# Layer-1 weight sums on GpSimd: positions 13 to 17 of a turn left out

## The chip, the core and the metric

One core of a Trainium2 chip runs the program. TensorE (PE in the profile, its weight loads PEld) does the products, VectorE (DVE), ScalarE (ACT) and GpSimd (POOL) do elementwise work, SyncE (SP) issues every transfer of the kernel. Each engine works through its own instructions in order. The metric is device time in microseconds (us), the median of several runs.

## The reference

Two layers on 8192 tokens of 768 features, 64 tokens to a graph.

```
# layer 0, 12 heads of 64
h    = x @ W                              # per head
attn = leaky(tanh(h)@w_src + (tanh(h)@w_dst)^T), masked by adj, softmax
fo   = elu(attn @ h + b)
gate = sigmoid(x @ H_w.T + H_b)
x    = layernorm(x + gate*fo + (1-gate)*x)
# layer 1, 6 heads of 128
q, k, v = x@Wq+bq, x@Wk+bk, x@Wv+bv
x = layernorm(x + softmax(masked q k^T / sqrt(128)) v @ Wf + bf)
```

## The kernel before, in words

The tokens are cut in 32 pairs of 128-token tiles. Layer 0 takes one pair in each *turn* p = 0 to 31. Its three large products of a pair, h, gate and v (v belongs to layer 1, but is made here), are each seven block products in the place of eight; the operands are sums of quarter blocks of x or of the weights. Layer 1 then takes the pairs two by two and makes q, k and the output product with 15 block products ("wide") in the place of 18; their weight operands are sums of 2 x 256-row blocks of Wq, Wk and Wf.

Those weight sums are made ahead, in layer 0, by `sum_weights` (L341). It is a generator: it loads a block to `wacc` (L354), loads another to `wadd` (L357), adds it on GpSimd (L361; L367 where a block is only negated), goes on so for each further block, and stores `wacc` to DRAM (L370), from where layer 1 loads it. There are 72 such chains (12 of the 15 sums, two halves, three matrices) with 132 additions or negations of 128x256 elements. `wacc` and `wadd` have one buffer each, so a load waits on SyncE for the addition before it, or for the landing of the store before it.

A turn has 21 *positions*, numbered from 0. Position n issues one block product to TensorE (`step`) and then what is planned at that position for the other engines; `was` plans for the older pair, `at` for the newer one. The items are h1 h2 u4 u3 h6 g1 h5 h7 g2 g6 h4 h3 g5 g7 v1 v2 g4 v6 g3 v5 v7 (u is the rest of the v product of the turn before). What other engines are given, as far as the prediction speaks of it; t1 and t0 are the two tiles:

- position 0, 3: transposes of the probabilities (L955); 1, 3: `residual` on GpSimd (L1006), which waits for ScalarE's gate
- 2, 5: attention products; 3, 6: their division on VectorE (L992, L993)
- 4, 7: gating on VectorE (L1011, L1016, L1018); 5, 8: statistics, with one small GpSimd power each (L322); 6, 9: the normalisation, and the store of x1 (L1027); 8: loads of x
- 11, 12: `products`: tanh, VectorE's product (L878), GpSimd's product (L879), for t1 and then t0
- 13, 14: `terms`: VectorE's reduction (L886) and three small transfers (L888, L891), and `with_bias`: GpSimd's addition (L902) and two transfers (L907, L908)
- 15, 16, 19: VectorE's sums of x1 (`value_sums`, L240 to L243, tile `sv_v`), the second of which (L241) is the operand of the product v6 at position 17
- 16, 18: logits on VectorE (L915), 18 and 20: masking and maximum (L931, L937, L938)
- 17: GpSimd's sums of the next pair's x (`x_sums`, the same lines L240 to L243, tile `sx_x`)

The additions of `sum_weights` are put among this in turns 2 to 30: after the acts of a position the generator is advanced once at even and twice at odd positions (L1188 to L1190). An addition comes three steps after its load. In this way they fall on all positions, and the work is done in turn 24.

In the trace a turn is told by its first product with the name `x_h` (h2, position 1). "Time 35.2 of a turn" is us after that.

Of the kernel before, what the change touches and what calls it, by code (L numbers as in the profile page):

```python
# [9 lines left out]
F32 = mybir.dt.float32  # L10
# [3 lines left out]
ALU = mybir.AluOpType  # L14
AX = mybir.AxisListType

P = 128
# [117 lines left out]
def kernel(  # L135
# [21 lines left out]
    nc = tc.nc  # L157
    NP = x.shape[0]
    NG = NP // 2
    SCALE = 1.0 / math.sqrt(E1)  # L160
    W2 = PAIR * P
# [8 lines left out]
    V, S, G, T = nc.vector, nc.scalar, nc.gpsimd, nc.tensor  # L170
# [134 lines left out]
    def step(job, i):  # L305
        job.product(i)
        flush()
        behind.append((job, i))
# [32 lines left out]
    def sum_weights(pool):  # L341

        for key, src in (("q", wq), ("k", wk), ("f", wf)):
            for n, (_, blocks, *_) in enumerate(WIDE):
                if blocks[0][2] > 0 and len(blocks) == 1:
                    continue
                for kc in range(2):

                    def block(k, f):
                        r0 = (2 * k + kc) * P  # L350
                        return src[r0 : r0 + P, f * W2 : (f + 1) * W2]

                    acc = pool.tile([P, W2], F32, tag="wacc", name=f"wacc_{key}{n}_{kc}", bufs=1)
                    nc.sync.dma_start(out=acc, in_=block(*blocks[0][:2]))  # L354
                    for k, f, sign in blocks[1:]:
                        t = pool.tile([P, W2], F32, tag="wadd", name=f"wadd_{key}{n}_{kc}_{k}{f}", bufs=1)
                        nc.sync.dma_start(out=t, in_=block(k, f))  # L357
                        yield
                        yield
                        yield  # L360
                        G.tensor_tensor(acc, acc, t, ALU.add if sign > 0 else ALU.subtract)  # L361
                    if blocks[0][2] < 0:
                        assert len(blocks) == 1
                        yield
                        yield
                        yield
                        G.tensor_scalar(acc, acc, -1.0, None, ALU.mult)  # L367
                    yield
                    yield
                    nc.sync.dma_start(out=wide_d[key][n][:, kc, :], in_=acc)  # L370
                    yield
                    yield

    def wide_place(key, n):
# [362 lines left out]
    def drain(*sides):  # L737
        for s in sides:
            for _ in s:
                pass  # L740
# [4 lines left out]
    with ExitStack() as ph, ExitStack() as ph_r:  # L745
        sb = ph.enter_context(tc.tile_pool(name="sb0", bufs=2))
# [346 lines left out]
            jobs["rows"] = rows  # L1093

        v_sums, carried = {}, {}
        summing = sum_weights(sb)
        for p in range(NP + 1):
            q = p - 1
            new, old = p < NP, 0 <= q < NP
# [84 lines left out]
            for pos, item in enumerate(turn):  # L1184
                step(jobs[item[0]], int(item[1:]))
                for act in plan.get(pos, ()):
                    act()
                if 2 <= p < NP - 1:  # L1188
                    for _ in range(1 + pos % 2):
                        next(summing, None)  # L1190
                if item[0] == "q":
                    jobs["rows"].ready(int(item[1:]) + 4)
            if p == NP - 2:
                drain(summing)
            if old:
                jobs["u"] = jobs["v"]
        flush()
# [3 lines left out]
    with ExitStack() as ph:  # L1201
        sb = pools["late"] = ph.enter_context(
            tc.tile_pool(name="sb1", bufs=2, reuse_waits="tile")
        )
# [42 lines left out]
        for g in range(1, NG):  # L1247
# [26 lines left out]
            p = 2 * g - 2  # L1274
# [7 lines left out]
        p = 2 * NG - 2  # L1282
# [66 lines left out]
```

## Time and profile before

| what | us |
|---|---|
| median of 4 runs (2899.89 to 2903.07) | 2901.36 |
| the profiled execution | 2899.93 |
| its span, first to last instruction | 2898.1 |
| TensorE busy (98% of the span) | 2843.1 |
| VectorE busy (67%) | 1936.2 |
| GpSimd busy (45%) | 1292.2 |
| ScalarE busy (37%) | 1060.4 |
| the 126 additions L361, by matrix q, k, f | 36.4, 36.1, 35.9 |
| TensorE waiting for L241 of VectorE, whole span | 8.6 in 9 waits |

Busy time is the time in which an engine ran instructions; "idle before" is the time for which it stood still, with the instruction whose end released it. The granted TensorE clock is 0.996 of full speed. Layer 0 takes about the first 1540 us, a turn some 46.

### The profile page before, as it was taken

The page shows a single profiled execution, that of the slowest core. Times are in us where ns is not written, and L with a number is a line of the kernel's source. Part 1 is how long each engine was busy: PE and PEld are TensorE (multiplying, and loading weights), DVE is VectorE, ACT ScalarE, POOL GpSimd, SP SyncE. Part 2 cuts the span into 40 slices and gives each one's busy share as a digit, 9 for nine tenths or more (in the row PEclk, how much of TensorE's full clock was granted, in tenths as well). Part 3 has the DMA queues.
Part 4 walks back from the last instruction along what each step waited for, and adds up shares of the span by engine and source line. Part 5 has one row for each costly group of instructions (what it writes and reads, how often), then busy time and mean ns, then how long its engine had stood idle before and what let it go on. Part 6 is the DMA issues. An engine that isn't in the chain of part 4 may idle for free.

```text
span 2898.1 us, 47864 instructions
## 1 busy us (share of the span) xinstructions
PE 2843.1 (98%) x18252; PEld 2074.7 (72%) x18252; DVE 1936.2 (67%) x3201; ACT 1060.4 (37%) x1896; POOL 1292.2 (45%) x1253
## 2 busy tenths in 40 slices
PE   7899999999999999999999999999999999999998
PEld 4566556666566655666668888888888888888886
DVE  6888788888878888887874545555545555554556
ACT  2344444444444444444433123333213333322332
POOL 2434454444535444333443454444545443444534
PEclk9999999999999999999999999999999999999999
DMA  5344444544444444333353434332334333233432
GB/s 175 119 156 149 149 142 144 159 146 147 143 153 147 140 148 134 120 121 104 121 201 84 124 101 110 106 92 75 87 81 111 110 101 91 72 84 95 110 88 74
DMA packets 321780, 348.73 MB, mean 120 GB/s; under 512 B 147856, under 2 KB 246672, under 8 KB 321552
## 3 DMA queue, kind: packets, MB, share of 16 engines
q1 hardware_dynamic: 321552, 345.66, 39.1%
q8 instruction: 146, 2.39, 0.4%
q14 instruction: 82, 0.67, 0.1%
HBM read 198.48 MB, written 122.29 MB: 111 GB/s over the span
## 4 chain that ended last, share of the span: by engine, by line
PE 82%; DVE 10%; DMA 3%; ACT 2%; issue 2%; POOL 1%; SPq 0%; POOLq 0%; DVEq 0%; ACTq 0%
PE z_k L442 9%; PE z_o L489 8%; PE z_q L442 8%; PE y_h L270 7%; PE y_g L270 6%; PE y_k L442 6%; PE y_v L270 6%; PE y_o L489 6%; PE y_q L442 5%; PE z_h L270 4%; PE z_v L270 3%; PE z_g L270 2%; PE x_g L270 2%; PE sp L545 2%; PE cp L629 2%
## 5 line engine op out<-in xcount | busy, mean ns | idle before, releaser
L569 ACT ACTIVATE sc<-sc 128x512 f32<-128x512 f32 x48 | 30.7, 639 | 615.2 <-DVE sc L566 615.2
L690 POOL TENSOR_TENSOR y<-y,bf_bc 128x768 f32<-128x768 f32 x64 | 114.7, 1814 | 290.1 <-DMA y<-x1d 290.1
L502 DVE TENSOR_TENSOR y<-y,z_o 128x256 f32<-128x256 f32 x320 | 127.3, 418 | 139.3 <-PE z_o L489 139.0
L489 PE MATMUL z_o<-wf,so 128*128 128x256 f32 x896 | 215.8, 383 | 1.6 <-DVE y L502 1.6
L442 PE MATMUL z_q<-xs,w_wq 128*128 128x256 f32 x896 | 213.5, 381 | 0.3 <-POOL xs L406 0.3
L406 POOL TENSOR_TENSOR so<-ctxT 128x256 f32<-128x256 f32 x224 | 159.8, 732 | 91.2 <-PE y_o L489 46.5
L442 PE MATMUL z_k<-xs,hw_wk 128*128 128x256 f32 x840 | 198.5, 379 | 0.0
L1006 POOL TENSOR_TENSOR x<-gate,x 128x768 f32<-128x768 f32 x64 | 119.6, 1869 | 162.4 <-ACT gate L1057 148.3
L442 PEld LDWEIGHTS z_q<-xs,w_wq 128*128 128x128 f32 x896 | 168.7, 190 | 24.3 <-POOL xs L406 0.7
L489 PEld LDWEIGHTS z_o<-wf,so 128*128 128x128 f32 x896 | 167.1, 190 | 26.0 <-DVE y L502 1.4
L322 POOL TENSOR_TENSOR rs_b<-ve_b,minus_half 128x1 f32<-128x1 f32 x64 | 40.4, 631 | 314.8 <-DVE ve_b L320 313.0
L879 POOL TENSOR_TENSOR th<-th,wsd 128x768 f32<-128x768 f32 x64 | 117.2, 1832 | 140.3 <-DVE th L878 140.3
L442 PEld LDWEIGHTS z_k<-xs,hw_wk 128*128 128x128 f32 x840 | 159.5, 190 | 21.7
L322 POOL TENSOR_TENSOR rs_a<-ve_a,minus_half 128x1 f32<-128x1 f32 x64 | 35.8, 560 | 305.7 <-DVE ve_a L320 305.7
L406 POOL TENSOR_TENSOR xs<-r,r 128x512 f32<-128x512 f32 x112 | 147.6, 1334 | 39.7 <-DMA r<-x1Td 22.5
L457 DVE TENSOR_TENSOR qT<-qT,z_q 128x512 f32<-128x512 f32 x96 | 66.0, 687 | 141.7 <-PE z_q L442 140.7
L270 PE MATMUL y_v<-wv,sv_v 128*128 128x384 f32 x384 | 136.3, 491 | 10.3 <-DVE sv_v L241 8.6
L270 PE MATMUL y_h<-w_wq,xT 128*128 128x384 f32 x384 | 136.5, 492 | 8.7 <-DMA w_wq<-in_w_dram 8.0
L457 DVE TENSOR_TENSOR kT<-kT,z_k 128x512 f32<-128x512 f32 x96 | 66.0, 688 | 112.5 <-PE z_k L442 110.4
L270 PE MATMUL y_h<-w_wq,sx_x 128*128 128x384 f32 x384 | 136.5, 492 | 4.2 <-ACT h L839 4.2
L270 PE MATMUL y_g<-hw_wk,sx_x 128*128 128x384 f32 x384 | 136.4, 492 | 2.5 <-DVE hw_wk L219 2.2
L270 PE MATMUL z_v<-wv,sv_v 128*128 128x384 f32 x384 | 137.5, 494 | 1.0 <-DVE v L869 1.0
(163 smaller groups left out, 6912.8 us busy)
## 6 DMA issues: line engine op xcount, KB each, us to landing
x<-in_x_dram SPq DMA_DIRECT2D x64, 384.0 KB, 3.7
dd<-dstd SPq DMA_DIRECT2D x128, 192.0 KB, 3.4
x1d<-x SPq DMA_DIRECT2D x64, 384.0 KB, 2.6
x1Td<-x1T SPq DMA_DIRECT2D x32, 768.0 KB, 4.2
vd<-v SPq DMA_DIRECT2D x64, 384.0 KB, 3.1
r<-x1Td SPq DMA_DIRECT2D x96, 256.0 KB, 3.5
v<-vd SPq DMA_DIRECT2D x384, 64.0 KB, 2.3
y<-x1d SPq DMA_DIRECT2D x64, 384.0 KB, 5.7
```

Of the source, the lines that this page charges most:

```text
L270: T.matmul(to[:, : self.n], lhsT, rhs, start=kc == 0 and not more, stop=kc == HK - 1, skip_group_check=more,)
L322: G.tensor_tensor(rstd, ve, minus_half, ALU.pow)
L406: G.tensor_tensor(t, self.of(x[0]), self.of(x[2]), x[1])
L442: T.matmul(b[:, half * W2 : (half + 1) * W2], w[:, kc, half * P : (half + 1) * P], x[:, kc, :], start=half == kc == 0 and not more, stop=k ...
L457: V.tensor_tensor(at, at, b.rearrange("p (h t) -> p h t", h=2), ALU.add if sign > 0 else ALU.subtract,)
L489: T.matmul(b[:, :W2], x[:, kc, :], w[:, kc, :], start=kc == 0 and not more, stop=kc == 1, skip_group_check=more,)
L502: V.tensor_tensor(at, at, self.banks[path][:, :W2], ALU.add if sign > 0 else ALU.subtract)
L545: T.matmul(self.sp_[gr * N : (gr + 1) * N, (i * 2 + a) * N : (i * 2 + a + 1) * N], qT[:, 2 * self.f + a, at], kT[:, 2 * self.f + a, at], s ...
L629: T.matmul(self.cp_[a][e, at], self.v_[rows, i, gr, e], self.scT_[rows, at], start=True, stop=True,)
L690: G.tensor_tensor(y, y, pools["bf"], ALU.add)
L879: G.tensor_tensor(th[:, 1, :], th[:, 1, :], wsd[:, 1, :], ALU.mult)
L1006: G.tensor_tensor(xp, st[t]["gate"], xp, ALU.mult)
```

## The change

`sum_weights` now asks before each addition whether it may: it stays in `while not (yield)` until the turn sends it true. The turn sends once at every position, and false at 13 to 17. The step after the addition issues the store, the next one the load of the following block; before, each of these came two steps later. A negation goes through the same loop. The first load is issued ahead of turn 0.

```diff
-                    for k, f, sign in blocks[1:]:
-                        t = pool.tile([P, W2], F32, tag="wadd", ...)
-                        nc.sync.dma_start(out=t, in_=block(k, f))
+                    for k, f, sign in blocks[1:] or [(None, None, -1)]:
+                        if k is not None:
+                            t = pool.tile([P, W2], F32, tag="wadd", ...)
+                            nc.sync.dma_start(out=t, in_=block(k, f))
                         yield
+                        while not (yield):
+                            pass
+                        if k is None:
+                            G.tensor_scalar(acc, acc, -1.0, None, ALU.mult)
+                        else:
+                            G.tensor_tensor(acc, acc, t, ALU.add if sign > 0 else ALU.subtract)
                         yield
-                        yield
-                        G.tensor_tensor(acc, acc, t, ALU.add if sign > 0 else ALU.subtract)
-                    if blocks[0][2] < 0:
-                        assert len(blocks) == 1
-                        yield
-                        yield
-                        yield
-                        G.tensor_scalar(acc, acc, -1.0, None, ALU.mult)
-                    yield
-                    yield
                     nc.sync.dma_start(out=wide_d[key][n][:, kc, :], in_=acc)
-                    yield
                     yield
...
-        summing = sum_weights(sb)
+        summing, summed = sum_weights(sb), False
+        next(summing)
...
-                if 2 <= p < NP - 1:
-                    for _ in range(1 + pos % 2):
-                        next(summing, None)
+                if 2 <= p < NP - 1 and not summed:
+                    try:
+                        summing.send(not 13 <= pos <= 17)
+                    except StopIteration:
+                        summed = True
...
-                drain(summing)
+                assert summed
```

Counted from the two programs, the 132 additions stand behind these positions:

| position | 0 | 1 | 2, 3 | 4 | 5, 6 | 7 | 8 | 9 | 10 | 11 | 12 | 13 to 17 | 18 | 19, 20 | last turn |
|---|---|---|---|---|---|---|---|---|---|---|---|---|---|---|---|
| before | 5 | 10 | 15 | 3 | 10 | 11 | 5 | 9 | 4 | 7 | 4 | 36 | 2 | 11 | 24 |
| after | 9 | 18 | 1 | 20 | 6 | 13 | 11 | 3 | 6 | 13 | 5 | 0 | 27 | 0 | 29 |

The numbers of additions, loads and stores are the same, and without those the order of every engine's instructions is unchanged.

More of the change, by code (lines that the diff above doesn't have):

```diff
@@ L354, in sum_weights @@
                     nc.sync.dma_start(out=acc, in_=block(*blocks[0][:2]))
-                    for k, f, sign in blocks[1:]:
-                        t = pool.tile([P, W2], F32, tag="wadd", name=f"wadd_{key}{n}_{kc}_{k}{f}", bufs=1)
-                        nc.sync.dma_start(out=t, in_=block(k, f))
+                    for k, f, sign in blocks[1:] or [(None, None, -1)]:
+                        if k is not None:
+                            t = pool.tile([P, W2], F32, tag="wadd", name=f"wadd_{key}{n}_{kc}_{k}{f}", bufs=1)
+                            nc.sync.dma_start(out=t, in_=block(k, f))
                         yield
-                        yield
-                        yield
-                        G.tensor_tensor(acc, acc, t, ALU.add if sign > 0 else ALU.subtract)
-                    if blocks[0][2] < 0:
-                        assert len(blocks) == 1
-                        yield
-                        yield
-                        yield
-                        G.tensor_scalar(acc, acc, -1.0, None, ALU.mult)
-                    yield
-                    yield
+                        while not (yield):
[4 more added lines that the diff above has]
+                            G.tensor_tensor(acc, acc, t, ALU.add if sign > 0 else ALU.subtract)
+                        yield
                     nc.sync.dma_start(out=wide_d[key][n][:, kc, :], in_=acc)
-                    yield
                     yield
```

## The prediction

> **What bounds the kernel now.** I read the shares, then TensorE's waits, then single turns. TensorE is busy for 98% of the span. Its waits between 120 and 1440 us, where the change acts:
>
> ```profile
> PE 2843.1 (98%) x18252; PEld 2074.7 (72%) x18252; DVE 1936.2 (67%) x3201; ACT 1060.4 (37%) x1896; POOL 1292.2 (45%) x1253
> ...
> PE y_v L270 <- DVE sv_v L241: 7.8, 8, 1.7
> ```
>
> So the product v6 waits for VectorE's second sum of x1 in eight turns. What the weight sums cost in all shows by the turn's length. The table by stretches has a turn without sums (number 29), and two with them (23 and 22):
>
> ```profile
> 1348.22:1393.83 45.61, 45.61 (x249) 27.68 (x247) 36.92 (x55) 20.01 (x33) 16.53 (x14) 1.00 0.34 113
> 1074.04:1119.72 45.68, 45.63 (x249) 27.72 (x247) 36.83 (x54) 20.13 (x33) 27.18 (x24) 1.00 0.46 148
> 1026.99:1074.04 47.05, 45.77 (x248) 27.68 (x247) 38.61 (x56) 20.00 (x33) 20.22 (x18) 1.00 0.47 147
> ```
>
> First the length, then PE, PEld, DVE, ACT, POOL. All turns from 25 on take 45.6 us. Turns 3 to 24 reach from 152.04 to 1165.78 us: 1013.74 - 22 x 45.60 = **10.5 us lost to the sums**. Turn 2 has one between its two L902 (0.73 us) ahead of a 1.36 us wait; I add 0.7. The sums thus cost 11.2 us, and no change of their places can bring more.
>
> Next, what makes v6 late. The timeline of turn 29, no sums (start, us, engine):
>
> ```profile
> 1376.48 1.81 POOL L879 TENSOR_TENSOR th<-th,wsd 128x768 f32<-128x768 f32 x1 [0.89 <-DVE th L878]
> ...
> 1378.25 3.34 POOL L902 TENSOR_TENSOR h<-h,b_bc 128x768 f32<-128x768 f32 x2
> ...
> 1380.70 1.31 DVE L240 TENSOR_TENSOR sv_v<-x1T 128x384 f32<-128x384 f32 x1
> ...
> 1381.53 1.33 POOL L240 TENSOR_TENSOR sx_x<-xT 128x384 f32<-128x384 f32 x1
> 1382.04 1.24 DVE L241 TENSOR_TENSOR sv_v<-sv_v,x1T 128x384 f32<-128x384 f32 x1
> ...
> 1383.42 2.17 PE L270 MATMUL y_v<-wv,sv_v 128*128 128x384 f32 x6
> ```
>
> VectorE's L240 ends 0.42 us after L902 (1381.59), its L241 0.42 after GpSimd's own L240: each finishes only when the GpSimd instruction beside it has ended. v6 starts 0.14 us after L241, at time 35.20 of the turn. So there is no slack: what delays L902 delays v6. Turn 17 has an addition at position 12, ahead of L902:
>
> ```profile
> 826.69 0.73 POOL L361 TENSOR_TENSOR wacc_f<-wacc_f,wadd_f 128x256 f32<-128x256 f32 x1
> ...
> 827.37 3.33 POOL L902 TENSOR_TENSOR h<-h,b_bc 128x768 f32<-128x768 f32 x2
> ...
> 830.65 1.32 POOL L240 TENSOR_TENSOR sx_x<-xT 128x384 f32<-128x384 f32 x1
> 831.15 1.23 DVE L241 TENSOR_TENSOR sv_v<-sv_v,x1T 128x384 f32<-128x384 f32 x1
> ```
>
> Its v6 starts at 832.53, time 36.02: 0.82 late. But turn 3, with an addition at position 11 between the two L879, is on time (187.25, time 35.21):
>
> ```profile
> 179.38 1.45 POOL L361 TENSOR_TENSOR wacc_q<-wacc_q,wadd_q 128x256 f32<-128x256 f32 x1
> 180.80 1.81 POOL L879 TENSOR_TENSOR th<-th,wsd 128x768 f32<-128x768 f32 x1
> 182.57 3.33 POOL L902 TENSOR_TENSOR h<-h,b_bc 128x768 f32<-128x768 f32 x2
> ...
> 186.35 0.56 DVE L241 TENSOR_TENSOR sv_v<-sv_v,x1T 128x384 f32<-128x384 f32 x1
> ...
> 194.69 0.73 POOL L361 TENSOR_TENSOR wacc_q<-wacc_q,wadd_q 128x256 f32<-128x256 f32 x1 [8.79 <-DMA wadd_q<-in_wq_dram]
> 195.38 1.31 POOL L240 TENSOR_TENSOR sx_x<-xT 128x384 f32<-128x384 f32 x1
> ```
>
> L902 ends 0.5 us late there too (185.90, time 33.86 against 33.37). But the addition of position 16 waits for its load 8.79 us, and **holds GpSimd's sums of x, queued behind it, away from VectorE's L241**, which takes 0.56 us in the place of 1.24. A hold of 2 us or more stands ahead of L240 in most turns with an addition at 15 or 16; the change takes it away.
>
> **The change, part by part.** Counts are those of the issue order; no instruction is added.
>
> (1) Removed: 36 additions at 13 to 17, and all old places. The 11.2 us go; each new place is priced in the turns of before that have the same one.
>
> (2) 13 additions at position 11 (7 before). L879 of t0 starts 0.47 us late (time 28.75 in turn 3, 28.28 in the row above), so do L902 and, with no hold, v6: 13 x 0.47 = **6.1 us**. Ends: 0 (turn 3) and 0.82 (turn 17). I take 0.47, since in every new turn GpSimd's L240 stands directly behind L902, as in turn 29.
>
> (3) 5 at position 12 (4 before): 0.75, between the addition's 0.73 and turn 17's 0.82: **3.8 us**. Ends 0 and 4.1.
>
> (4) Late loads. Position 11's load is issued at 9, behind the x1 store that waits for ScalarE (SyncE, time 22.6), and in seven turns behind the landing of the store of position 8 as well. Of the six additions at 11 of turns 3 to 24, two waited:
>
> ```profile
> 1056.68 0.73 POOL L361 TENSOR_TENSOR wacc_f<-wacc_f,wadd_f 128x256 f32<-128x256 f32 x1 [1.50 <-DMA wadd_f<-in_wf_dram]
> ```
>
> and 0.3 us in turn 14. Behind it are queued L879, both L902 and the x sums; VectorE's L886, SyncE's L907 and v6 wait for these. Mean (1.5 + 0.3) / 6 = 0.3; 13 x 0.3 = **3.9 us**. Ends: none late, 0; all by the mean of the two, 0.9, 11.7.
>
> (5) Pairs at positions 1 and 4: 12 turns. The first pushes L1006 of t0 onto VectorE's L1011, the second falls on L1016. In turn 8 (additions at 388.92 and 391.91) these take 1.83 and 1.37 us in the place of 1.34 and 0.96; the normalisation, and behind it on ScalarE the tanh, come later, and L878 starts at time 24.98, 0.28 later than 24.50 plus the 0.2 by which this turn was already late. Turns 14, 16 and 19 show the same 0.28, and L879 follows. 12 x 0.28 = **3.4 us**, ends 0 and 3.4. The eight additions at 4 without one at 1 fall behind L1006, as in turn 15 (0.04, nothing).
>
> (6) 9 at position 0, one round trip (2.2 us) behind the addition of 18, so some 2.1 us before the next turn's first x_h, where VectorE runs L915. It matters because L938 of t0 ends at 2.28 of the next turn, and ScalarE's exponentials and gate, VectorE's divisions and TensorE's second transposes follow without slack: turn 24, with an addition 1.67 us before its x_h, ends L938 0.45 late and is 0.47 longer. Turn 18, with one 1.96 us before, shows 0.01. I take 0.05: **0.5 us**; ends 0 and 4.1.
>
> (7) 27 at position 18, directly behind GpSimd's L243, which ends at time 40.46. The 0.73 us lie beside VectorE's L937 (40.5 to 41.5), a reduction that takes 0.95 us with or without GpSimd beside it. **0**. Without that cover it would fall on L938, by turn 24 0.45 us each: upper end 12.2.
>
> (8) The rest: positions 5 to 10 stand beside VectorE's small operations, and their successors on GpSimd (L322) come 2 us or more later; 0. SyncE's stores and loads at 12 to 14 stand between the two tiles' small transfers; turn 18 has the same two loads there, and its logits did not wait. The 17 stores at 19 and loads at 20 stand ahead of the loads of xT and adj, as in turn 8, where xT had 25 us to spare. The early first load is one 0.33 us issue: 0.
>
> The sum: 6.1 + 3.8 + 3.9 + 3.4 + 0.5 = 17.7, less 11.2: **+6.5 us**. The profiled execution would take 2899.9 + 6.5 = 2906.4 (its span 1.8 less); the median, 1.4 above it, **2907.9**.
>
> The row for the contention is L240's end 0.42 us after L902's. The Trainium skill (SBUF — State Buffer, "Who interferes with whom") says that a VectorE instruction with two SBUF inputs contends with any GpSimd instruction that reads SBUF, and that the second to issue blocks until the first has finished. That speaks against the change: emptied positions still hold L902 and the x sums, which block just as well. By that rule alone the 18 additions at 11 and 12 would each cost their whole 0.73 us, 13.1 in the place of 9.9; I keep the rows.
>
> **Rivals.** (A) Loads come in time and pairs cost nothing: 6.1 + 3.8 + 0.5 - 11.2 = -0.8, **2900.6**. For it: four of six additions at 11 did not wait. Against: four turns of four show the pair's 0.28. (B) The other side, not slower but faster: the x sums begin late without a hold. The place is GpSimd's L240, the price all of (2), (3) and (5): 3.9 + 0.5 - 11.2 = -6.8, **2894.6**. It decides from L240 at time 34.5 or later, when VectorE's L241 is through. What could do it is a late xT load, which moves behind the store of position 19; against it: in turn 8 it landed at time 8.0, 25 us early. (C) The additions of 18 start late, and fall on L938: 17.7 + 12.2 - 11.2 = +18.7, **2920**. Against: their loads are issued at 11 to 16; the margin to L938 is only 0.4 us.
>
> **How the numbers follow.** The forecast's own range is 2902 to 2914 (the late loads of (4) between 0 and 0.8 each), chance 0.58; A 0.22, B 0.08, C 0.12. A measurement of this kernel can tell about 0.2%, 5.8 us. Above 2907.2 lie 0.36 of the forecast and C: slower 0.48. Within: 0.22 of it and A: 0.44. Faster: B, 0.08. The range for 8 in 10 reaches into A and part of C: 2899 to 2918.
>
> **What would show it.** Right: in turns with an addition at 11 or 12 v6 starts 0.5 to 0.8 us after 35.2, with GpSimd's L240 directly behind L902; turns without (12, 21) take 45.6; L241 is still what TensorE waits for most. (4) is right if some L361 ahead of L879 still wait for a load, (5) if L878 slips by 0.28, (7) if L938 beside position 18 stays at 0.96. Wrong: v6 on time in those turns, or waits at the transposes in every turn.

## The result, and the profile after

The changed kernel takes **2905.3 us** (median of 33 runs, 2902.11 to 2907.9) against 2900.77 of the kernel before (53 runs beside it on the same chips): a ratio of 1.0015, 95% interval 1.001 to 1.002. It is slower by 4.5 us: the interval leaves out 1, so the loss is clear of noise, though it is below the 0.2% that the prediction took for the limit of what can be told. The forecast was 2907.9, range 2899 to 2918; of its three outcomes (slower, within 0.2%, faster) "within", held at 0.44, came true, and not "slower", held at 0.48.

The profiled execution took 2907.7 us. Its page has the same shares; VectorE's busy time is 17 us longer, TensorE's 2 us:

```profile
PE 2845.5 (98%) x18252; PEld 2074.2 (71%) x18252; DVE 1952.9 (67%) x3201; ACT 1059.7 (36%) x1896; POOL 1282.3 (44%) x1253
```

What TensorE waits for between 120 and 1440 us (total, times, longest):

```profile
PE y_v L270 <- DVE sv_v L241: 13.2, 23, 1.2
PE pTp L951 <- DVE fo L989: 0.5, 3, 0.2
```

Before, v6 waited in 8 turns, up to 1.7 us; now it waits in 23, at most 1.2. The changed file is four lines shorter up to here, so L898 is the old L902, L875 the old L879, L874 L878, L911 L915, L934 L938, L951 L955, L989 L993, and L365 is the addition. Turns 3, 18, 17, 12 and 30 by stretches (length, then PE, PEld, DVE, ACT, POOL):

```profile
150.51:196.59 46.08, 45.77 (x248) 27.70 (x247) 38.07 (x55) 20.02 (x33) 20.70 (x18) 1.00 0.44 133
566.87:612.94 46.07, 45.86 (x249) 27.61 (x247) 37.85 (x55) 20.05 (x34) 19.29 (x18) 1.00 0.49 153
798.00:844.71 46.71, 45.76 (x249) 27.70 (x247) 38.81 (x55) 19.98 (x33) 20.16 (x19) 1.00 0.45 141
844.71:890.98 46.27, 45.75 (x249) 27.70 (x247) 38.06 (x55) 20.01 (x33) 19.90 (x19) 1.00 0.43 139
1399.55:1445.16 45.61, 45.61 (x249) 27.70 (x248) 36.91 (x55) 20.01 (x33) 16.54 (x14) 1.00 0.30 97
```

Turn 30 has no sums left and takes 45.61, as before. Turn 3 has an addition at 11, turn 18 one at 12; these lose 0.47 and 0.67. Turns 17 and 12 lose by what the sum had put at nothing. Turn 18 in the timeline:

```profile
874.74 0.72 POOL L365 TENSOR_TENSOR wacc_k<-wacc_k,wadd_k 128x256 f32<-128x256 f32 x1
...
875.42 3.33 POOL L898 TENSOR_TENSOR h<-h,b_bc 128x768 f32<-128x768 f32 x2
...
878.70 1.31 POOL L240 TENSOR_TENSOR sx_x<-xT 128x384 f32<-128x384 f32 x1
879.19 1.23 DVE L241 TENSOR_TENSOR sv_v<-sv_v,x1T 128x384 f32<-128x384 f32 x1
...
880.57 1.85 PE L270 MATMUL y_v<-wv,sv_v 128*128 128x384 f32 x5 [0.52 <-DVE sv_v L241]
```

GpSimd's L240 stands directly behind L898, VectorE's L241 ends 0.42 us after it, and v6 starts at time 35.86, 0.66 late. Turn 17 shows the first thing that was missed, an addition of position 10 that waits 3.81 us for its load, with L875 queued behind it:

```profile
824.00 0.73 POOL L365 TENSOR_TENSOR wacc_k<-wacc_k,wadd_k 128x256 f32<-128x256 f32 x1 [3.81 <-DMA wadd_k<-in_wk_dram]
824.68 1.81 POOL L875 TENSOR_TENSOR th<-th,wsd 128x768 f32<-128x768 f32 x1
825.11 2.19 DVE L874 TENSOR_TENSOR th<-th,wsd 128x768 f32<-128x768 f32 x1 [0.91 <-ACT th L873]
```

Turn 12 shows the second. The addition of position 18 of turn 11 waits for its load and falls beside VectorE's L911, which takes 1.99 us (1.52 without):

```profile
563.54 0.78 POOL L365 TENSOR_TENSOR wacc_k<-wacc_k,wadd_k 128x256 f32<-128x256 f32 x1 [1.82 <-DMA wacc_k<-in_wk_dram]
563.64 1.99 DVE L911 TENSOR_TENSOR att<-dd,sd 128x768 f32<-128x768 f32 x1
```

### The profile page after: what moved, and what is told of

Its sections match the earlier page's. It is cut to its first block, busy times and chain, and to the rows that moved or that the text cites. A ratio compares the mean times of both kernels' runs of the same rounds, so it can differ in the third digit from the quotient of the medians.

```text
span 2905.9 us, 47839 instructions
## 1 busy us (share of the span) xinstructions
PE 2845.5 (98%) x18252; PEld 2074.2 (71%) x18252; DVE 1952.9 (67%) x3201; ACT 1059.7 (36%) x1896; POOL 1282.3 (44%) x1253
## 4 chain that ended last, share of the span: by engine, by line
PE 82%; DVE 11%; ACT 3%; DMA 2%; issue 1%; POOL 1%; SPq 0%; POOLq 0%; DVEq 0%; ACTq 0%
PE z_o L485 8%; PE z_k L438 8%; PE z_q L438 8%; PE y_h L270 8%; PE y_v L270 6%; PE y_k L438 6%; PE y_o L485 6%; PE y_q L438 5%; PE y_g L270 5%; PE z_h L270 4%; PE z_v L270 4%; DVE sd L882 3%; PE z_g L270 2%; PE x_g L270 2%; PE cp L625 2%; PE sp L541 2%
## 5 line engine op out<-in xcount | busy, mean ns | idle before, releaser
L322 POOL TENSOR_TENSOR rs_b<-ve_b,minus_half 128x1 f32<-128x1 f32 x64 | 40.4, 631 | 314.2 <-DVE ve_b L320 312.4
L322 POOL TENSOR_TENSOR rs_a<-ve_a,minus_half 128x1 f32<-128x1 f32 x64 | 35.9, 561 | 315.4 <-DVE ve_a L320 307.5
L875 POOL TENSOR_TENSOR th<-th,wsd 128x768 f32<-128x768 f32 x64 | 117.2, 1831 | 124.9 <-DVE th L874 124.9
L270 PE MATMUL z_h<-w_wq,sx_x 128*128 128x384 f32 x384 | 137.6, 495 | 0.6 <-DVE w_wq L216 0.6
```

The lines of the kernel that those rows point to most:

```text
L270: T.matmul(to[:, : self.n], lhsT, rhs, start=kc == 0 and not more, stop=kc == HK - 1, skip_group_check=more,)
L322: G.tensor_tensor(rstd, ve, minus_half, ALU.pow)
L875: G.tensor_tensor(th[:, 1, :], th[:, 1, :], wsd[:, 1, :], ALU.mult)
```

## The experiments

Eleven runs. Medians compare only within runs on one chip (the kernel before stands at 2900.6, 2900.7 and 2897.4 in the three sets), so the ratio is given; it is estimated from all the runs and lies up to 0.0006 off the quotient of the medians. Beside it stands, from each one's trace, by how much turns 3 to 29 exceed 27 x 45.60 us, and the length of turn 2. What lies outside these turns differs by some 3 us either way between executions. The column is one execution each: turns 3 to 24 of the kernel before, which three dose runs below contain unchanged, exceed by 10.5, 12.4, 11.9 and 10.7 us in the four traces, so a difference under 2 us in it shows nothing.

| kernel | median, us | ratio to before, 95% interval | turns 3 to 29 over 45.60 | turn 2 |
|---|---|---|---|---|
| before | 2900.77 | 1 | 10.6 | 48.3 |
| after | 2905.3 | 1.0015 (1.001 to 1.002) | 17.8 | 48.1 |
| e1_all: nothing closed | 2895.45 | 0.9986 (0.9977 to 0.9994) | 8.4 | 47.6 |
| e2_no11: 11 to 17 closed | 2900.37 | 1.0001 (0.9993 to 1.001) | 11.5 | 50.8 |
| e3_hold: after, x sums held | 2894.65 | 0.9978 (0.9969 to 0.9986) | 6.5 | 48.2 |
| e4_bhold: before, x sums held | 2898.55 | 0.9993 (0.9984 to 1.0002) | 11.3 | 48.3 |
| e7_noload: after without loads | 2903.35 | 1.0013 (1.0004 to 1.0022) | 15.4 | 48.1 |
| e8_cheap: cheap positions alone | 2895.36 | 0.9983 (0.9974 to 0.9992) | 3.1 | 49.5 |
| e10_cheap3: the same from turn 3 | 2889.2 | 0.9973 (0.9964 to 0.9982) | 2.7 | 47.6 |
| e11_cheap3_hold: and x sums held | 2882.66 | 0.9955 (0.9942 to 0.9967) | -1.8 | 47.6 |

### The closing undone, and made wider

```diff
-                        summing.send(not 13 <= pos <= 17)
+                        summing.send(True)                      # e1_all
...
-                        summing.send(not 13 <= pos <= 17)
+                        summing.send(not 11 <= pos <= 17)       # e2_no11
+                        if pos == 6:
+                            summing.send(True)
```

> The changed kernel with the turn sending true at every position, so the pace and the spacing of loads and stores stay those of the change and only the closing of positions 13 to 17 is undone. Additions per position 8 3 9 6 7 8 3 9 5 6 6 7 6 6 8 2 9 8 4 5 7, done in turn 24. Theory (the time is set by what stands ahead of or beside GpSimd's L902 and x sums, and additions at 15 and 16 that wait for their load hold the x sums off): fewer additions at 11 (7 for 13), holds are back, six turns fewer are touched; about the time of the kernel before, 2899 to 2903. Rival (the closer spacing, or one step a position, is what costs): stays at 2904 to 2907.

> The changed kernel with positions 11 to 17 closed in the place of 13 to 17, and a second step at position 6 so that the sums still end in turn 29 (14 13 0 5 17 6 16 8 4 8 13 additions at 0 to 10, 28 at 18). Theory: the 18 additions ahead of L902 are gone, which took 6.0 + 3.4 us and 0.8 for late loads in the trace; 13 in the place of 6 stand at position 10, where late loads took 0.4 us each, and 7 pairs in the place of 12 at 0.28 us: -10.2 + 2.8 - 1.4, about 2896 (2892 to 2900), faster than the kernel before. VectorE's L241 keeps GpSimd's L240 beside it (1.23 us). Rival (what counts is only that 13 to 17 are closed, or the number of turns with sums): 2903 to 2907.

Measured: 2895.45 and 2900.37. **The change has two parts of opposite sign.** Its new pace (one step a position, the store and the next load two steps earlier) with nothing closed gains 5 us; closing 13 to 17 then costs 9.9. The traces have 9.4 of this in turns 3 to 29; of the gain of the pace they show 2.2, little more than the spread between executions. Both theories had e1_all too slow. Closing 11 and 12 as well gives 4.9 back, half of what was forecast. By the traces turns 3 to 29 gain 6.3, and turn 2 loses 2.6, where an addition waits 4.57 us for its load ahead of both L875. The additions go to position 10 and before, and wait for loads there; the text had priced that at position 10 alone. In turn 6 an addition of position 7 waits 8.66 us, with GpSimd's small power L322 queued behind it:

```profile
315.91 0.73 POOL L365 TENSOR_TENSOR wacc_q<-wacc_q,wadd_q 128x256 f32<-128x256 f32 x1 [8.66 <-DMA wadd_q<-in_wq_dram]
...
316.64 0.55 POOL L322 TENSOR_TENSOR rs_a<-ve_a,minus_half 128x1 f32<-128x1 f32 x1
```

The normalisation behind L322 is late, L898 ends at 35.95 in the place of 33.37, and the turn takes 48.19.

### The loads taken away

```diff
+        acc = pool.tile([P, W2], F32, tag="wacc", name="wacc", bufs=1)
+        nc.sync.dma_start(out=acc, in_=wq[:P, :W2])
+        t = pool.tile([P, W2], F32, tag="wadd", name="wadd", bufs=1)
+        nc.sync.dma_start(out=t, in_=wq[:P, W2 : 2 * W2])
         for key, src in (("q", wq), ("k", wk), ("f", wf)):
...
-                    acc = pool.tile(...)
-                    nc.sync.dma_start(out=acc, in_=block(*blocks[0][:2]))
...
-                            t = pool.tile(...)
-                            nc.sync.dma_start(out=t, in_=block(k, f))
```

> The changed kernel without the loads of the weight sums: both buffers are loaded once ahead of the turns, and the 132 additions and 72 stores stand at their places but add the same block over and over, so layer 1 gets other weights. The theory: what goes is only the lateness of loads, about 2.4 us at position 10, 0.8 at position 11 and 0.9 at position 18 in after: 2905.3 - 4.1 = 2901.2, range 2899.5 to 2903; turns 7, 8, 16 and 17 lose 0.7 each, turns 12 and 21 go to 45.60. Rival: the lateness is covered or the place costs, and the time stays at 2904 to 2906.

Measured: 2903.35, 2 us below after, between the two expectations. The ratios, 1.0013 and 1.0015, cannot tell the two kernels apart; the traces have turns 3 to 29 shorter by 2.4. The turns say why (turns 12 and 17 here):

```profile
566.16:611.79 45.63, 45.63 (x249) 27.74 (x248) 37.40 (x55) 20.02 (x33) 19.26 (x18) 1.00 0.38 126
796.72:842.58 45.86, 45.78 (x249) 27.74 (x248) 37.97 (x55) 19.98 (x33) 20.63 (x19) 1.00 0.36 119
```

Turn 17 falls from 46.71 to 45.86, turn 12 from 46.07 to 45.63. Added up over the nine turns that become shorter, from one execution of each kernel: 1.9 us for late loads at position 10 (turns 7, 8, 16, 17), 0.9 at 11 (turns 19, 22, 23), 0.9 at 18 (turns 12, 21). But 1.3 us come back in turns 5, 11, 14, 20, 25 and 29, and some 0.5 in turns 7 and 16, which 1.9 is already less by. There the turn before has an addition at 18, and the next one is planned at position 0 of the turn itself. With its load late (2.6 us after the first behind turn 10 of after) the second lies beyond L934 of t1; without loads it follows at once and falls on it (1.25 us in the place of 0.96). **A late load costs ahead of L875 and saves behind the x sums.**

### The price of a place by itself

Into the turns 25 to 30 of the kernel before, which have no sums and take 45.60, single multiplications that wait for nothing were put (0.61 us each, where an addition of the sums takes 0.73):

```diff
+                for _ in range({25: (11,), 26: (12,), 27: (10,), 28: (1, 4), 29: (18,), 30: (5,)}.get(p, ()).count(pos)):
+                    dose = sb.tile([P, W2], F32, tag="wacc", name=f"dose_{p}_{pos}", bufs=1)
+                    G.tensor_tensor(dose, wsd[:, 1, :W2], wsd[:, 1, :W2], ALU.mult)
```

> The kernel before, with one GpSimd multiplication of 128x256 that waits for no load put into each of the turns 25 to 30, which have no weight sums and take 45.60 us each; its product is used by nothing. Turn 25 has it at position 11, 26 at 12, 27 at 10, 28 one each at 1 and 4, 29 at 18, 30 at 5. The theory (the place alone costs, as priced from the turns of after): 46.07 for turn 25, 46.31 for 26, 45.60 for 27, 45.88 for 28, 45.60 for 29 and for the turn that follows it, 45.60 for 30. The rival to the late loads of position 10: the place itself costs there, and turn 27 takes 46.0 or more without any load. Of position 18: 46.07 in the turn after 29 if the addition falls on the subtraction L938 even when it is not late.

> As the kernel before it, other places: turn 25 at position 13 (between the two bias additions L902), 26 at 14 (between the second of them and GpSimd's sums of x), 27 at 1 alone, 28 at 4 alone, 29 at 11 and 12, 30 two at 14. The theory: 46.33 for turn 25 (the whole 0.73 on the way of L902); 45.4 for 26 and 45.38 for 30, less than 45.60, since the sums of x begin 0.7 and 1.4 us later and VectorE's second sum of x1 has less or nothing beside it; 45.60 for 27 and 28; 46.8 for 29 (0.47 and 0.73). Rival: an instruction at 14 blocks VectorE's second sum as the sums of x do, and 26 takes 45.6 to 46.3; positions 1 or 4 alone cost 0.1 to 0.28.

| placed at | turn's length | cost | expected cost |
|---|---|---|---|
| 11 | 45.97 | 0.37 | 0.47 |
| 12 | 46.18 | 0.58 | 0.71 |
| 13, between the two L902 | 46.17 | 0.57 | 0.73 |
| 10 | 45.60 | 0 | 0 |
| 18 (and the next turn) | 45.61, 45.60 | 0 | 0 |
| 5; 4 alone | 45.60; 45.62 | 0 | 0 |
| 1 and 4 | 45.64 | 0.04 | 0.28 |
| 1 alone, in the turn after the one with 14 | 45.47 | not of position 1, see below | 0 |
| 14; two at 14 | 45.52; 45.53 | -0.1 | -0.2 |
| 11 and 12 | 45.58 | 0 | 1.2 |

Position 10 costs nothing by itself: its price in after is the lateness of loads. An instruction at 14, ahead of the x sums, even gains, since it holds them off VectorE's L241 (0.85 us in the place of 1.24). The gain of the next turn, with a dose at 1, is of the same source: its L938 of t0 ends at time 1.96 (the turn begins at 1257.30), before that dose has run:

```profile
1258.30 0.96 DVE L938 TENSOR_TENSOR att<-att,mx 128x768 f32<-128x768 f32 x1
```

In turn 29 of the kernel before, undisturbed, it ends at 2.28 (the turn begins at 1348.22):

```profile
1349.54 0.96 DVE L938 TENSOR_TENSOR att<-att,mx 128x768 f32<-128x768 f32 x1
```

So one at 14 gains 0.08 in its own turn and 0.13 in the next, together the 0.2 that were expected; what position 1 costs alone this run does not show. The pair at 1 and 4 comes out small, as far as the rows tell because the dose is shorter: L1011 and L1016 take 1.72 and 1.25 us beside it, 1.83 and 1.37 beside the additions of after's turn 26, which is 0.28 long.

The last row was the surprise: two instructions ahead of L902 cost nothing, where one costs 0.4 to 0.6. That turn (29) in the timeline:

```profile
1378.79 0.60 POOL L1193 TENSOR_TENSOR dose<-wsd 128x256 f32<-128x256 f32 x1
...
1379.36 3.65 POOL L902 TENSOR_TENSOR h<-h,b_bc 128x768 f32<-128x768 f32 x2
...
1380.87 0.59 DVE L240 TENSOR_TENSOR sv_v<-x1T 128x384 f32<-128x384 f32 x1
...
1381.50 1.92 DVE L241 TENSOR_TENSOR sv_v<-sv_v,x1T 128x384 f32<-128x384 f32 x1
```

VectorE's L240 is issued at 1380.87, just before the first L902 ends (some 1.68 us after 1379.36, at 1381.04), and is through 0.42 us after that end. L241 is then blocked by the second L902, not by GpSimd's L240. In an undisturbed turn L240 is issued at time 32.48, after the first L902 has ended at 31.72, so it sits out the second, and L241 sits out one more. If this is right, two at 12 must cost less than one:

> The kernel before, with GpSimd multiplications of 128x256 that wait for no load (0.61 us each, product used by nothing) in turns 25 to 30: turn 25 one at position 12, 26 two at 12, 27 three at 12, 28 two at 13, 29 two at 11, 30 one at 11 and one at 12. The theory after turn 29 of the dose run before it, where 11 and 12 together cost nothing: VectorE's two sums of x1 each end 0.42 us after the end of a GpSimd instruction, and what counts is which two ends these are. Without doses they are the ends of the second L902 and of GpSimd's L240. Where the first L902 ends after VectorE's L240 is issued (time 32.5; undisturbed it ends at 31.7), they are the ends of the first and the second L902, and nothing more of L240. So: 46.2 for one at 12, 45.4 to 45.6 for two at 12, 46.0 to 46.2 for three (the second L902 is 1.8 late, 0.5 more than a GpSimd L240), 45.4 to 45.6 for two at 13 and for 11 with 12, and 46.5 to 46.8 for two at 11, since there L879 is late, VectorE's L886 waits for it and its L240 is issued only after the first L902. Rival, each addition costs its time ahead of v6: 46.2, 46.8, 47.4, 46.8, 46.6, 46.6.

Measured in the order of that text: 46.17, 45.92, 46.60, 45.90, 46.66, 45.58. Two at 12 cost 0.32 where one costs 0.57; two at 13 cost 0.30; two at 11 cost 1.06, three at 12 cost 1.00. Against the rival, a second instruction at 12 or 13 makes the turn shorter, and two at 11 cost their full time, as the theory has it. Three sizes (two at 12, three at 12, two at 13) are 0.3 to 0.6 higher than forecast. The two doses with the gap between them take 1.31 us, where I had put 1.2, and the two L902 behind them take 3.64 in the place of 3.34: the second ends 1.6 late, 0.3 more than a GpSimd L240 lasts. Two at 12 (turn 26):

```profile
1240.31 1.31 POOL L1193 TENSOR_TENSOR dose<-wsd 128x256 f32<-128x256 f32 x2
...
1241.58 3.64 POOL L902 TENSOR_TENSOR h<-h,b_bc 128x768 f32<-128x768 f32 x2
...
1242.75 0.94 DVE L240 TENSOR_TENSOR sv_v<-x1T 128x384 f32<-128x384 f32 x1
1243.72 1.92 DVE L241 TENSOR_TENSOR sv_v<-sv_v,x1T 128x384 f32<-128x384 f32 x1
1245.19 1.31 POOL L240 TENSOR_TENSOR sx_x<-xT 128x384 f32<-128x384 f32 x1
```

L241 ends at 1245.64, 0.42 us after the second L902 (1245.22), before GpSimd's L240 has done half.

### GpSimd's sums of x held back

A GpSimd instruction of 128x1, which reads VectorE's second sum of x1, was put ahead of the x sums, so that these cannot start before L241 has ended; in after (e3_hold) and in the kernel before (e4_bhold):

```diff
         def x_sums(p):
+            if p >= 4:
+                held = small.tile([P, 1], F32, tag="rstd", name=f"held_{p}")
+                G.tensor_tensor(held, B[p - 2][6][:, 0, :1], minus_one, ALU.mult)
             operands, steps = sums_of(G, sbr, "sx", xTs[p], f"x{p}")
```

> The changed kernel with a hold made on purpose: ahead of GpSimd's sums of x, from turn 3 on, one GpSimd instruction of 128x1 that reads a column of VectorE's second sum of x1 (its result is not used). GpSimd's L240 can then not stand beside VectorE's L241. Theory: L241 takes 0.56 us in the place of 1.23, v6 starts 1.14 us after L902's end and never before 35.05, so the additions at 11 and 12 cost 0 to 0.2 in the place of 0.5 to 0.75, and every turn gains 0.15; VectorE's later chain is earlier by up to 0.3 us. About -14 - 4: 2887 (2883 to 2893). Rival (the hold does not matter; the additions cost because they delay L902, whatever follows): v6 still late by 0.5 to 0.75 in those turns, 2903 to 2908.

> The kernel before with the same hold. Theory: of its 10.5 us most stand in turns where the x sums ran directly behind L902; these go, and 0.15 in each turn: about 2890 (2886 to 2894), and the change would then bring next to nothing on top: within 3 us of e3. Rival: no gain, 2899 to 2903; or, if positions 13 to 17 cost in themselves, clearly slower than e3.

Measured: 2894.65 and 2898.55. e3_hold gains 10.7 us on after, so rival B's mechanism is real, but both stay 8 us above what was expected. e4_bhold's 2 us are not clear of noise (the interval reaches 1.0002), and its text's rival, no gain, is nearer: in its trace turns 3 to 24, where additions held the x sums in most turns already, exceed by 12.4 us, no less than without the hold. With the x sums held in both, the change is by the medians 3.9 us faster than the kernel before, not slower. e3_hold's waits of TensorE:

```profile
PE pTp L951 <- DVE fo L989: 3.5, 20, 0.2
PE y_v L270 <- DVE sv_v L241: 1.4, 2, 1.2
```

v6 hardly waits any more, and L241 takes 0.56 us. In the place of that wait 20 turns now have one of 0.17 at the next turn's transposes, the end of VectorE's chain L242, L911, L934 and the exponentials. Turn 9 of e3_hold:

```profile
459.55 0.56 DVE L241 TENSOR_TENSOR sv_v<-sv_v,x1T 128x384 f32<-128x384 f32 x1
...
460.33 1.00 POOL L240 TENSOR_TENSOR sx_x<-xT 128x384 f32<-128x384 f32 x1
460.50 1.25 DVE L242 TENSOR_TENSOR sv_v<-x1T 128x384 f32<-128x384 f32 x1
...
461.67 2.24 DVE L911 TENSOR_TENSOR att<-dd,sd 128x768 f32<-128x768 f32 x1
```

The held x sums lie on L242 (1.25 us; 0.88 in the undisturbed turn). A turn of the kernel before without sums still gains: 45.38 in turns 25 to 28 of e4_bhold.

### Cheap positions alone, and with the hold

```diff
-                if 2 <= p < NP - 1 and not summed:
+                if 3 <= p < NP - 1 and not summed:              # e10_cheap3, e11_cheap3_hold; not e8_cheap
                     try:
-                        summing.send(not 13 <= pos <= 17)
+                        summing.send(pos in (0, 1, 2, 5, 6, 7, 8, 9, 18, 19, 20))
+                        if pos in (2, 6, 19):
+                            summing.send(True)
```

e11_cheap3_hold has the edit of e3_hold too.

> The changed kernel with additions at positions 0, 1, 2, 5 to 9 and 18 to 20 alone, and a second step at 2, 6 and 19, so that the 132 additions still end in turn 29 (counted: 13 at 0, 1 at 1, 22 at 2, 20 at 5, 8 at 6, 7 at 7, 19 at 8, 2 at 9, 27 at 18, 13 at 20; no turn with a pair at 1 and 4). The theory: of the 17.8 us by which after's turns 3 to 29 exceed 45.60 only the late loads ahead of 18 and some at 0 and 8 are left, about 3: 2905.3 - 15 = 2890, range 2887 to 2895, faster than both kernels. Rival: loads come late at 8 and 9, with GpSimd's small power L322 and both L879 queued behind them as in the run with 11 to 17 closed, and the time is 2896 to 2902.

> As the run with the cheap positions alone (2895.36), but the sums begin in turn 3, not 2, and end in turn 30. The theory: turn 2 took 49.52 there, since its addition waited 5.7 us for its load ahead of both L879; without sums it takes 47 to 48.3, and one more turn at the end costs 0: 2892.5 to 2895. Rival: turn 2 is set by something else, and the time stays at 2895 to 2896.

> The same, and GpSimd's sums of x wait for VectorE's second sum of x1, as in the other run with a hold. If v6's wait alone bound the turn, each of turns 3 to 30 would go from 45.6 to 45.38: 2894 - 6 = 2888. The theory after the two runs with a hold, that VectorE's chain from its sums of x1 to L938 and the next turn's transposes has no slack either: the held sums of x and the additions of 18 behind them fall on L242, L915 and L938, TensorE waits 0.17 at the transposes in most turns, and the time is 2892 to 2896, no better than without the hold.

Measured: 2895.36, 2889.2 and 2882.66 (the last of 5 runs, the others of 11). The turns 3 to 29 of e8_cheap cost 3.1 us in all, as forecast; its median is 0.4 above the range, and turn 2 is 1.4 longer than in after (49.5 against 48.1); starting in turn 3 takes that away (47.6). The chip of the last two has the kernel before 3.3 lower, so e10_cheap3's 2889.2 answers to some 2892.5 beside the expectation, and e11_cheap3_hold's 2882.66 to some 2886.

e11_cheap3_hold went against the theory that I had formed from e3_hold and with the other reading in that text (2888), and is the **fastest of all: 14.8 us below the kernel before**. Its waits, and its turn 12:

```profile
PE y_v L270 <- DVE sv_v L241: 1.3, 2, 0.7
PE pTp L951 <- DVE fo L989: 0.5, 3, 0.2
```

```profile
561.76:607.15 45.39, 45.39 (x249) 27.80 (x247) 37.13 (x55) 20.02 (x33) 20.23 (x18) 1.00 0.40 129
```

Most turns take 45.38 with an addition at 18 in them. So VectorE's chain to the transposes does have slack when the x sums are held, just little. In e3_hold the second L898 ends between times 33.5 and 34.7, mostly after 34.0, and the transposes wait in 20 turns and more; in e11_cheap3_hold it ends between 33.2 and 33.7 in all turns but one, and they wait in six, 0.05 to 0.18. As these two runs have it, the late L898, and not the held sums by themselves, used the slack up. That is a reading of two traces, not tested by a run of its own, and it is not all: in e11_cheap3_hold turn 4 waits 0.17 behind an L898 that ended at 33.46, and turn 10 does not behind one at 33.71.

## Why the prediction was right

The sum was +6.5 us; 4.5 were measured by the medians, and in the traces turns 3 to 29 exceed 45.60 by 17.84 where the prediction had 17.7 for all new places. That agreement is partly luck, as the terms show, and closer than one execution can tell.

- (1) The old places' 11.2 us: 10.5 in turns 3 to 24 stand, the lowest of four executions (10.5 to 12.4). Of the 0.7 in turn 2 only 0.2 came (48.32 to 48.13), since an addition stands ahead of the L902 there again, between the two L875 (1.45 us).
- (2) Position 11: right. Turns 3 and 5 take 46.08 and 46.07, 0.47 each. (The reading "28.28" is 28.26 by the row that it points at, so 0.49 in the place of 0.47, 0.3 us in the sum.)
- (3) Position 12: 0.66 to 0.71 in turns 9, 11, 18, 20 and 27, 3.4 in all against 3.8.
- (4) Late loads at position 11 is **the term that failed**: 3.9 forecast, 0.7 measured in after's trace (0.9 by e7_noload). The mean of two waits in six turns of before was carried to 13 turns without asking which of them would delay L879. Six of the 13 additions waited, and the three that waited 0.4 to 0.7 us cost nothing. Turns 3 and 5 show why, the first with no wait, the second with one:

```profile
177.54 1.17 DVE L874 TENSOR_TENSOR th<-th,wsd 128x768 f32<-128x768 f32 x1 [1.08 <-ACT th L873]
...
177.85 1.44 POOL L365 TENSOR_TENSOR wacc_q<-wacc_q,wadd_q 128x256 f32<-128x256 f32 x1
...
269.98 1.16 DVE L874 TENSOR_TENSOR th<-th,wsd 128x768 f32<-128x768 f32 x1 [1.08 <-ACT th L873]
...
270.74 0.98 POOL L365 TENSOR_TENSOR wacc_q<-wacc_q,wadd_q 128x256 f32<-128x256 f32 x1 [0.42 <-DMA wadd_q<-in_wq_dram]
```

  Both additions end 0.58 us after VectorE's L874 does. An addition on time takes 1.44 us there, not 0.73, and the wait only shortens that. In turns 19, 22 and 23 it starts at L874's end or later, takes 0.72 to 0.73, and ends 0.3, 0.2 and 0.1 later than an addition on time would.
- (5) Pairs: right, 0.28 (turn 26: 45.88).
- (6) Position 0: 0.1 to 0.4 in four turns of nine, 0.9 in all against 0.5. The addition came 2.3 to 3.8 us behind that of 18, not 2.2; where it started 1.4 to 1.8 us ahead of the next turn's x_h it could fall on VectorE's L243 (0.80 us at the end of turn 28, 0.54 free) and delay L934.
- (7) Position 18: 25 of 27 cost nothing, beside the reduction, as forecast. Two came 1.5 and 1.8 us late (turns 20 and 11), fell on L911 and cost the next turn 0.47 each; nearly rival C's mechanism, in 2 turns and not 27. So turns 12 and 21, named as a sign with 45.6, took 46.07.
- (8) "Positions 5 to 10 ... 0" **failed for position 10**: the place is free (the dose), the loads are not. All six additions there waited, 1.65 to 3.85 us, and four turns lost 2.4 by it (0.7 in turn 7, 0.45 in 8 and 16, 0.8 in 17). It is not the x1 store of (4): the load is issued ahead of that store, directly behind the two loads of x, as in turn 17 (which begins at 798.00):

```profile
816.07 2.02 SPq L759 DMA_DIRECT2D x<-in_x_dram  x2
818.18 0.38 SPq L358 DMA_DIRECT2D wadd_k<-in_wk_dram  x1
821.52 0.33 SPq L1023 DMA_DIRECT2D x1d<-x  x1
```

  In the six turns it landed 0.3 us after the second load of x (1.2 in one), 3.5 to 5.7 us after its own issue, where the loads for position 11 took 2.1 to 4.5.

The miss of (4), 3.2 too much, and those of (6), (7) and (8), 0.4, 0.9 and 2.4 too little, nearly cancel, and so the sum held. One reading of the range does not come out: with no late loads the forecast is 2904.0, not the 2902 given as its lower end.

Of the rivals, A (loads in time, pairs free) fell on the pairs and on the loads of position 10. B (x sums late without a hold) did not happen by itself, but the hold showed its mechanism: with it after is faster than before.

The reason given for the loss stands: closing 13 to 17 (9.9 us between e1_all and after) moves additions from places that hold the x sums to places that delay L902 with the x sums directly behind. That turns 25 to 29 have sums too is not the cause: e8_cheap's sums end in turn 29 as well, and its turns 3 to 29 lose 3.1. The Trainium skill (SBUF — State Buffer, "Summary: rules for kernel authors") says that of a VectorE instruction with two inputs in SBUF, the on-chip memory, and a GpSimd one that reads SBUF the second to issue blocks until the first has finished. The dose runs agree: L240 and L241 each end 0.42 us after the end of a GpSimd instruction. But the estimate by that rule alone, each addition at 11 and 12 at its whole 0.73, is too high: they cost 0.47 and 0.69, and a dose at 11 with one at 12 nothing.

Left open: what in the new pace makes e1_all 5 us faster than before. Its turns 3 to 29 are shorter by 2.2 and turn 2 by 0.7; its traced execution took 2898.79, 3.3 more than its median, so the rest cannot be read from that trace. A version with additions at 14, which the dose shows to gain, was not tried.

## What to carry to other kernels

Price an instruction by what it makes the next engine wait for, not by its own length: the same 0.6 us cost 0.58, 0 or less than 0 according to where it stood and which end of a GpSimd instruction VectorE then met. When instructions are moved, move their loads in the account too, and ask of every load, not only of the suspicious one, whether it lands before its reader's new place, and what the reader would have waited for anyway. And when the first contended wait is taken away, test it in a turn that is clean otherwise: in e4_bhold the hold looked useless, in e11_cheap3_hold it was worth 6.5 us.

## What the runs showed of the hardware

More work ahead can cost less. VectorE's two additions each end 0.42 us after a GpSimd instruction's end, so the time goes in steps with the order of the ends: one multiplication at 12 cost 0.57 us, two 0.32, one at 11 with one at 12 nothing. The other way round, GpSimd's addition behind VectorE's L874 ends 0.6 us after it, whether its load came in time or 0.7 us late. An instruction of 0.19 us that makes GpSimd wait some 1.1 us shortened each clean turn by 0.22 (45.60 to 45.38).
